# Window attention and a Fourier layer in one pipeline: mode products split around the value product, modes loaded behind them, the next image loaded in two halves

## The chip, the cores and the metric

The kernel runs on one core of a Trainium2 chip. The metric is the time of one execution in microseconds on the device, as a median of several runs; lower is better. Everything is float32.

## The reference

The input is 32 images of 56 x 56 tokens with 128 channels. Two residual layers follow each other.

```python
# group norm without scale, 32 groups of 4 channels, over a whole image
def _gn(v, G=32, eps=1e-5): ...

# layer 0: shifted-window attention, windows of 7 x 7, 4 heads
x = x + attention(_gn(x))       # qkv, scores + bias + mask, softmax, values, projection

# layer 1: Fourier layer and a feed-forward net
def _forward_fourier(x, w0, w1):
    x_fty = dct(x along the width)                       # 56 -> the first 32 modes
    out_y = einsum('bixy,ioy->boxy', x_fty[..., :32], w0)    # one 128 x 128 product per mode
    xy = idct(out_y, back to 56)
    # ... the same along the height with w1 gives xx
    return xx + xy
x = x + relu(_forward_fourier(_gn(x)) @ W1 + b1) @ W2 + b2   # 128 -> 512 -> 128
```

## The kernel before

The program is unrolled. It goes through `cycle`s; one cycle handles one row of eight windows of an image (8 rows per image), and beside it the work of older rows and of the Fourier layer of the image before. `fourier(cycle)` gives the images in that layer with a number `c`; the text calls `c` modulo 8 the row. The row's parts on TensorE in order of time:

```python
def fourier(cycle):
    b, c = divmod(cycle - CONV_BEGIN, NWR)          # CONV_BEGIN = 11, NWR = 8
    return [(images[b - k], c + k * NWR) for k in (1, 0) if 0 <= b - k < NB]

# one cycle of the steady state
halves_first(cycle, norm)      # attn_qk; load_modes for this row; ff_in; softmax division
if not has_ff(cycle):          # only row 3 has no feed-forward group
    half_columns(cycle)        # transforms or mode products
eighths(cycle)                 # attn_values of row cycle-3 (L493)
quarters(cycle)                # attn_scores (L424), then modes_back (L709)
full(cycle)                    # attn_transpose of two rows (L468, even cycles), next image's groups (L269)
halves_last(cycle, norm)       # attn_v (L402); half_columns if has_ff; next_begin; ff_out; attn_project
```

What `half_columns` does depends on the row: row 0 transforms along the width (L636), rows 1 and 2 along the height (L636), row 3 holds the four groups of mode products of the height (`mix(im, False, g)`, `w1sb`), rows 4 and 5 two groups each of the width (`mix(im, True, g)`, `w0sb`). The modes come back through a DRAM scratch: `load_modes` and `modes_back` stand in rows 4 and 5 for the height, in 6 and 7 for the width.

```python
def half_columns(cycle):
    for im, c in fourier(cycle):
        ...
        elif c == 3:
            for g in range(4):
                mix(im, False, g)
        elif c in (4, 5):
            for g in (2 * c - 8, 2 * c - 7):
                mix(im, True, g)

def mix(im, width, g):
    ...
    pz = conv_bank()
    # 8 products of one mode each (L670), into one PSUM bank
    z = work.tile([P, 4, C], F32, tag="z", name="z", bufs=3)
    nc.scalar.copy(z.rearrange("p k c -> p (k c)"), pz)                    # L678
    for u in range(2):
        nc.sync.dma_start(im.zscr[width][:, u, 4 * g : 4 * g + 4], z[...])  # L680

def load_modes(im, width, g):
    zT = work.tile([P, 4, C], F32, tag="zT", name="zT", bufs=2)
    nc.sync.dma_start(zT[:, : n // 4], im.zscr[width][l0 : l0 + n]...)     # L691, needs all four mixes
```

PSUM has eight banks, four for the attention (`attn_bank`, tag `pa`) and four for the Fourier layer (`conv_bank`, tag `pc`). In each row the attention takes its banks for queries, keys, values, scores and transposes in turn:

```python
def attn_max(r):      # VectorE maximum (L442), then on GpSimd a = a - mx (L443)
def attn_divide(r):   # VectorE sum (L454), reciprocal (L456), then on GpSimd a = a * rs (L457)
def attn_transpose(im, i, r):
    for hf in range(2):
        pt = attn_bank()
        # 4 transposes of a_sb[r % 3] into pt (L468)
        if hf: nc.scalar.copy(aT, src)             # L476
        else:  nc.vector.tensor_copy(aT, src)      # L478
def attn_values(im, i, r):
    po = [attn_bank(), attn_bank()]
    # products (L493), then po[1] + bias by VectorE in three pieces (L524), po[0] + bias by ScalarE (L526)
def attn_scores(im, i, r):
    ps = [attn_bank(), attn_bank()]
    # products (L424), then a = ps + bias and mask by VectorE, twice (L432)
```

The next image is loaded where `next_begin` calls `image_begin` (row index 3 of the attention, which is row 0 of the Fourier layer), 28 chunks in all, into one of two buffers:

```python
def load_image(b):
    t = big.tile([TC, NCH, C], F32, tag="xl", name="xl", bufs=2)
    h = NCH // 2
    for n0, n1 in ((0, h), (h, NCH)):
        for a, e, p, src in chunks_of(x, b, n0, n1):
            nc.sync.dma_start(t[p, a:e], src)
    return t
```

Its first transposes stand two rows later (`image_groups`, the first half of the chunks in row 2, the second in row 3). The order of the four compute engines is that of the program; the order of DMAs on the SyncE queue (SP) is left to the scheduler, which works from what is ready.

Of the kernel before, what the change touches and what calls it, by code (L numbers as in the profile page):

```python
# [31 lines left out]
NCH = NT // TC  # L32
# [16 lines left out]
def swin_fourier_kernel(  # L49
# [20 lines left out]
    nc = tc.nc  # L70
    NB = x.shape[0]
# [14 lines left out]
    def conv_bank():  # L86
        return bank("pc", 4)
# [3 lines left out]
    def chunks_of(t, b, n0, n1):  # L91

        tok = t[b].rearrange("h w c -> (h w) c")
        wrap = (S - SS) // 2
        if n0 < wrap:
            e = min(n1, wrap)
            part = tok[SS * S + n0 * TC : SS * S + e * TC].rearrange("(n p) c -> p n c", p=TC)
            yield n0, e, slice(0, TC), part
        if n0 <= wrap < n1:
            yield wrap, wrap + 1, slice(0, S), t[b, S - 1].unsqueeze(1)  # L100
            yield wrap, wrap + 1, slice(S, TC), t[b, 0].unsqueeze(1)
        if n1 > wrap + 1:
            a = max(n0, wrap + 1)
            t0 = (2 * a + SS) % S * S
            part = tok[t0 : t0 + (n1 - a) * TC].rearrange("(n p) c -> p n c", p=TC)
            yield a, n1, slice(0, TC), part
# [5 lines left out]
            nc.tensor.matmul(dst[ps], lhsT=lhsT[:, ps], rhs=rhs, start=start, stop=stop)  # L112


    def load_image(b):
        t = big.tile([TC, NCH, C], F32, tag="xl", name="xl", bufs=2)
        h = NCH // 2
        for n0, n1 in ((0, h), (h, NCH)):
            for a, e, p, src in chunks_of(x, b, n0, n1):
                nc.sync.dma_start(t[p, a:e], src)  # L120
        return t

    xls = {0: load_image(0)}


# [28 lines left out]
    with nc.allow_non_contiguous_dma(reason="relative position bias, once"):  # L154
# [4 lines left out]
        for ix in range(WS):  # L159
            src = bass.AP(  # L160
                rpb_rev.tensor, rpb_rev.offset + WS - 1 - ix, [[span, NH * span], [1, WS]]
            )
# [42 lines left out]
    with nc.allow_non_contiguous_dma(reason="constant, once"):  # L205
        for blk in range(8):
# [4 lines left out]
            src = idct_h.rearrange("p (h r) -> p h r", r=4)[modes, :, 2 * li : 2 * li + 2]  # L211
# [39 lines left out]
    def image_begin(b):  # L251
        im = Image()
        im.b = b
        im.x = xls.pop(b) if b in xls else load_image(b)
        im.xw, im.aT = {}, {}
        im.st = small.tile([P, NWR, 6], F32, tag="st0", name="st0", bufs=2)
        im.part = small.tile([TC, 2, C // 4, NWR], F32, tag="part", name="part", bufs=1)
        im.scr = dram.tile([S, S, C], F32, tag="scr", name="scr", bufs=2)
        return im
# [401 lines left out]
    def mix(im, width, g):  # L661

        y, wmix = (im.yw, w0sb) if width else (im.yh, w1sb)
        if g == 0:
            im.zscr[width] = dram.tile([S, 2, NM // 2, C], F32, tag="zscr", name="zscr", bufs=3)
        pz = conv_bank()
        for c in range(4):
            for u in range(2):
                k = 8 * g + 2 * c + u
                nc.tensor.matmul(  # L670
                    pz[u * JP : (u + 1) * JP, c * C : (c + 1) * C],
                    lhsT=y[:, k * S : k * S + JP],
                    rhs=wmix[:, k],
                    start=True,
                    stop=True,
# [4 lines that stand above are left out]
            nc.sync.dma_start(  # L680
                im.zscr[width][:, u, 4 * g : 4 * g + 4], z[u * JP : u * JP + S]
            )
# [5 lines left out]
    def load_modes(im, width, g):  # L688
        l0, n = LINES[g]
        zT = work.tile([P, 4, C], F32, tag="zT", name="zT", bufs=2)  # L690
        nc.sync.dma_start(  # L691
            zT[:, : n // 4],
            im.zscr[width][l0 : l0 + n].rearrange("(m r) u k c -> (r u k) m c", r=4),
        )
        im.zT[width, g] = zT
# [114 lines left out]
    images = {}  # L810

    def row(r):
        return (images[r // NWR], r % NWR) if 0 <= r < NB * NWR else (None, 0)

    def fourier(cycle):

        b, c = divmod(cycle - CONV_BEGIN, NWR)
        return [(images[b - k], c + k * NWR) for k in (1, 0) if 0 <= b - k < NB]

    def back_groups(c):  # L820

        if c in (4, 5, 6, 7):
            return [(c >= 6, c % 2 * 2 + j) for j in range(2)]
        return []

    def halves_first(cycle, norm):
        last, j = row(cycle - 4)
        if last:
            sums = attn_sums(last, j)
            next(sums)  # L830
        im, i = row(cycle)
        if im:
            attn_qk(im, i, False)
        for im, c in fourier(cycle):
            for width, g in back_groups(c):
                load_modes(im, width, g)
        next(norm)
        if last:
            next(sums)
        for im, c in fourier(cycle):  # L840
            if c == 0:
                im.stats = fourier_stats(im)
                im.cols = {}
                next(im.stats)
                load_columns(im, 0)
                load_columns(im, 1)
        for im, c in fourier(cycle):
            if c in FF_AT:
                ff_in(im, FF_AT.index(c))
        for im, c in fourier(cycle):  # L850
            if c == 0:
                next(im.stats)
        if row(cycle - 1)[0]:
            attn_divide(cycle - 1)

    def has_ff(cycle):
        return any(c in FF_AT for _, c in fourier(cycle))

    def half_columns(cycle):
        for im, c in fourier(cycle):  # L860
            if c == 0:
                for g in range(4):
                    transform(im, True, g)
            elif c in (1, 2):
                for g in (2 * c - 2, 2 * c - 1):
                    transform(im, False, g)
                    if c == 1:
                        load_columns(im, g + 2)
            elif c == 3:
                for g in range(4):  # L870
                    mix(im, False, g)
            elif c in (4, 5):
                for g in (2 * c - 8, 2 * c - 7):
                    mix(im, True, g)

    def quarters(cycle):
        im, i = row(cycle)
        if im:
            attn_scores(im, i, cycle)
        for im, c in fourier(cycle):  # L880
            for width, g in back_groups(c):
                modes_back(im, width, g)
# [22 lines left out]
    def last_out(cycle):  # L905
        for im, c in fourier(cycle):
            if c in FF_AT:
                ff_out(im, FF_AT.index(c))

    def halves_last(cycle, norm):  # L910
        im, i = row(cycle)
        if im:
            attn_v(im, i, cycle)
        if has_ff(cycle):
            half_columns(cycle)
        next_begin(cycle)
        next(norm)
        im, j = row(cycle - 3)
        if im:
            last_out(cycle)  # L920
            attn_project(im, j)
        if row(cycle)[0]:
            attn_exp(cycle)
        next(norm)

    def next_begin(cycle):
        b, i = divmod(cycle, NWR)
        if b + 1 < NB and i == 3:
            images[b + 1] = image_begin(b + 1)

# [37 lines left out]
    def nothing():  # L970
        while True:
            yield

    ET = mybir.EngineType
    with tc.manual_schedule(engines={ET.PE, ET.Activation, ET.DVE, ET.Pool}):
        images[0] = image_begin(0)
        for i in range(0, NWR, 2):
            image_groups(images[0], i)
        for _ in image_norm(images[0]):
            pass  # L980
        norm = nothing()
        for cycle in range(NB * NWR + CONV_BEGIN + FF_AT[-1] - NWR + 1):
            if cycle < CONV_BEGIN:
                first_rows(cycle, norm)
            else:
                halves_first(cycle, norm)
                if not row(cycle - 3)[0]:
                    half_columns(cycle)
                    last_out(cycle)
                    quarters(cycle)  # L990
                    continue
                if not has_ff(cycle):
                    half_columns(cycle)
                eighths(cycle)
                quarters(cycle)
                if row(cycle)[0] and cycle % 2:
                    attn_max(cycle)
                full(cycle)
                halves_last(cycle, norm)
            b, i = divmod(cycle, NWR)  # L1000
            norm = nothing()
            if i == NWR - 2 and b + 1 < NB:
                norm = image_norm(images[b + 1])
                next(norm)
# [62 lines left out]
```

## Time and profile before

| | |
|---|---|
| time, median of 3 | 3709.89 us (3704.5 to 3718.54) |
| span of the profiled execution | 3721.3 us |
| busy: TensorE / VectorE / ScalarE / GpSimd | 96% / 59% / 57% / 37% |
| mean granted TensorE clock | 0.993 |
| DMA, mean over the span | 105 GB/s |
| one image in the middle (row 0 to row 0) | about 115 us, from 1800.1 to 1915.7 us |

In the profile's lines PE is a matmul on TensorE, PEld its weight load, DVE VectorE, ACT ScalarE, POOL GpSimd, and SPq the queue of DMAs that SyncE issues. Each line of the timeline gives the start in us, the duration, the engine, the line of the kernel (L468), the operation, what is written and read, and in brackets the idle time of the engine before it and what ended it. A line of waits gives the waiting engine and tile, the releaser, the total in us, how often, and the longest. "issue" stands for idle time that no semaphore explains. The row of an instruction is found from its kind: `w1sb` is row 3, `dct_w` row 0, and so on.

### The profile page before, as it was taken

What the parts mean: (1) busy time and instruction counts of PE and PEld (TensorE: products, weight loads), DVE (VectorE), ACT (ScalarE), POOL (GpSimd) and SP (SyncE); (2) the same over time, 40 slices, a digit from 0 to 9 for tenths busy, and PEclk for the clock granted to TensorE, in tenths of its full rate; (3) what the DMA queues carried; (4) which work ended last, traced back from release to release, by engine and by line L of the source; (5) the groups of instructions that cost most, each with busy time, mean ns of one, the idle gap of its engine ahead of it and who ended that gap; (6) DMA issues with size and microseconds to landing.
All of it is one profiled execution on the core that took longest, in us unless ns stands there. A gap on an engine that the chain in (4) does not pass through costs nothing.

```text
span 3721.3 us, 161472 instructions
## 1 busy us (share of the span) xinstructions
PE 3575.8 (96%) x72064; PEld 2850.6 (77%) x72064; DVE 2209.7 (59%) x4738; ACT 2139.4 (57%) x4044; POOL 1371.3 (37%) x1421
## 2 busy tenths in 40 slices
PE   7899999999999999999999999999999999999999
PEld 5777777777777777778777877777777777777776
DVE  6765666565665666665656665566556666565641
ACT  4565556555555655556555565555555565655544
POOL 5443333343333333333333334333333334343321
PEclk9999999999999999999999999999999999999999
DMA  4334433444433343334334343433433433443333
GB/s 112 96 103 108 110 99 101 107 112 107 112 97 106 106 112 106 105 94 108 106 104 109 92 119 102 104 103 100 110 105 107 112 103 96 108 113 101 91 106 105
DMA packets 687350, 390.30 MB, mean 105 GB/s; under 512 B 39967, under 2 KB 657600, under 8 KB 686400
## 3 DMA queue, kind: packets, MB, share of 16 engines
q1 hardware_dynamic: 686045, 379.65, 37.7%
q8 instruction: 567, 9.29, 1.0%
q14 instruction: 127, 1.04, 0.1%
q10 hardware_dynamic: 611, 0.32, 0.0%
HBM read 218.29 MB, written 161.48 MB: 102 GB/s over the span
## 4 chain that ended last, share of the span: by engine, by line
PE 83%; DMA 7%; issue 2%; DVE 2%; POOL 2%; ACT 2%; SPq 1%; POOLq 0%; ACTq 0%; DVEq 0%
PE pc L112 34%; PE pa L112 13%; PE pa L402 6%; PE pa L468 6%; PE pc L636 5%; PE pa L424 4%; PE pc L709 4%; PE pc L670 4%; PE pa L493 4%; DMA zT<-zscr 4%; PE pa L269 2%; DMA zscr<-z 2%; POOL xl L300 2%; DMA out_dram<-res 1%; DVE a L432 1%
## 5 line engine op out<-in xcount | busy, mean ns | idle before, releaser
L457 POOL TENSOR_TENSOR a<-a,rs 128x784 f32<-128x784 f32 x256 | 389.7, 1522 | 1265.4 <-DVE rs L456 731.2
L112 PE MATMUL pc<-wff,hid 128*64 128x128 f32 x12544 | 745.2, 274 | 1.3 <-ACT hid L754 1.0
L112 PE MATMUL pc<-xf,wff 128*64 128x512 f32 (+2 forms) x3584 | 718.2, 539 | 0.6 <-DVE xf L720 0.6
L112 PEld LDWEIGHTS pc<-wff,hid 128*64 128x64 f32 x12544 | 707.8, 138 | 7.9 <-ACT hid L754 4.3
L778 DVE TENSOR_TENSOR res<-pc,res 128x512 f32<-128x512 f32 (+3 forms) x257 | 144.1, 571 | 910.9 <-issue 463.0
L443 POOL TENSOR_TENSOR a<-a,mx 128x784 f32<-128x784 f32 x256 | 389.8, 1522 | 662.8 <-DVE mx L442 623.8
L754 ACT ACTIVATE hid<-pc,b1sb 128x512 f32<-128x512 f32 (+2 forms) x896 | 538.3, 635 | 94.0 <-PE pc L112 91.9
L112 PEld LDWEIGHTS pc<-xf,wff 128*64 128x64 f32 x3584 | 286.0, 137 | 361.5 <-issue 281.1
L373 ACT ACTIVATE q<-pa,bqkv 128x392 f32<-128x392 f32 x256 | 149.7, 585 | 452.6 <-PE pa L112 451.0
L112 PE MATMUL pa<-xw,wn 128*64 128x392 f32 (+1 forms) x2048 | 393.9, 499 | 0.6 <-DVE a L432 0.6
L409 ACT COPY v<-pa 128x512 f32<-128x512 f32 x256 | 151.4, 591 | 269.6 <-PE pa L402 269.5
L742 POOL TENSOR_TENSOR res<-res,b2sb 128x512 f32<-128x512 f32 (+2 forms) x256 | 264.6, 1039 | 106.4 <-DMA res<-scr 96.9
L390 DVE TENSOR_SCALAR k<-pa,heads,bqkv 128x392 f32<-128x392 f32 x245 | 167.9, 685 | 213.4 <-ACT k L382 174.9
L300 POOL TENSOR_TENSOR xl<-xl,bproj 112x512 f32<-112x512 f32 (+1 forms) x256 | 287.1, 1144 | 0.0
L449 ACT ACTIVATE a<-a 128x784 f32<-128x784 f32 x256 | 222.2, 868 | 111.9 <-POOL a L443 109.7
L402 PE MATMUL pa<-wn,xw 128*64 128x128 f32 x4096 | 284.8, 281 | 0.2 <-issue 0.2
L468 PE MATMUL pa<-ident,a 113*113 113x113 f32 x2048 | 243.9, 272 | 39.6 <-ACT oT L526 38.1
L493 PEld LDWEIGHTS pa<-aT,v 49*32 49x32 f32 x16384 | 172.0, 105 | 139.0 <-issue 69.4
L432 DVE TENSOR_TENSOR a<-pa,bm 128x392 f32<-128x392 f32 x512 | 264.3, 558 | 16.3
L468 PEld LDWEIGHTS pa<-ident,a 113*113 113x113 f32 x2048 | 218.6, 181 | 60.7 <-issue 43.9
L112 PE MATMUL pa<-wproj,oT 128*64 128x128 f32 (+1 forms) x3584 | 249.0, 274 | 0.4 <-DVE oT L524 0.4
L454 DVE TENSOR_REDUCE sm<-a 128x16 f32<-128x784 f32 x256 | 245.8, 960 | 5.8 <-ACT a L449 4.9
(89 smaller groups left out, 5586.6 us busy)
## 6 DMA issues: line engine op xcount, KB each, us to landing
zscr<-z SPq DMA_DIRECT2D x512, 112.0 KB
htok<-scr SPq DMA_DIRECT2D x256, 196.0 KB
zT<-zscr SPq DMA_DIRECT2D x192, 256.0 KB
res<-scr SPq DMA_DIRECT2D x160, 256.0 KB
out_dram<-res SPq DMA_DIRECT2D x160, 256.0 KB
scr<-xl SPq DMA_DIRECT2D x128, 224.0 KB
xl<-in_x_dram SPq DMA_DIRECT2D x32, 784.0 KB
xl<-in_x_dram SPq DMA_DIRECT2D x32, 672.0 KB
```

The source lines that it names most:

```text
L112: nc.tensor.matmul(dst[ps], lhsT=lhsT[:, ps], rhs=rhs, start=start, stop=stop)
L300: nc.gpsimd.tensor_tensor(piece, piece, bproj.unsqueeze(1).to_broadcast([TC, e - a, C]), ALU.add)
L402: nc.tensor.matmul(pv[hs, j * C : (j + 1) * C], lhsT=im.xw[i][:, w * WT : w * WT + JP], rhs=im.w[:, 2 * C : 3 * C], start=True, stop=True,)
L432: nc.vector.tensor_tensor(a[:, 2 * hp : 2 * hp + 2, :, 0:WT].rearrange("p u w j -> p w u j"), ps[hp][:, :RT].rearrange("p (w u j) -> p w u ...
L443: nc.gpsimd.tensor_tensor(a3, a3, mx.unsqueeze(2).to_broadcast([P, 2 * NWR, WT]), ALU.subtract)
L449: nc.scalar.activation(a3, a3, AF.Exp)
L454: nc.vector.tensor_reduce(sm, a3, axis=AX.X, op=ALU.add)
L457: nc.gpsimd.tensor_tensor(a3, a3, rs.unsqueeze(2).to_broadcast([P, 2 * NWR, WT]), ALU.mult)
L468: nc.tensor.transpose(pt[:PW, h * P : h * P + PW], a[:PW, h, 2 * hf : 2 * hf + 2].rearrange("p w j -> p (w j)")[:, :PW], ident[:PW, :PW],)
L493: nc.tensor.matmul(po4[u][h * HD : (h + 1) * HD, 2 * f + e], lhsT=v[ks, 2 * f + e, h * HD : (h + 1) * HD], rhs=im.aT[i][f][ks, h, e * JP : ...
L742: nc.gpsimd.tensor_tensor(res[:m, c0:c1], res[:m, c0:c1], b2sb[:m].unsqueeze(1).to_broadcast([m, c1 - c0, C]), ALU.add,)
L754: nc.scalar.activation(hf[:, :n], ph[:, :n], AF.Relu, bias=b1sb[:, f : f + 1])
```

## The change

Three things are done. First, in the one row without a feed-forward group (row 3) only two of the four mode products stay ahead of the attention's values and scores; the other two move behind the value product (`attn_v`), so that the copies and stores of z come in two batches. Second, `load_modes` of the next row is written right behind the mode products, ahead of the feed-forward output and the projection with their stores, instead of at the beginning of the next row. Third, the next image's load is cut: the first half at the old place, the second half a row later.

```diff
-    def load_image(b):
+    def load_part(t, b, k):
+        h = NCH // 2
+        for a, e, p, src in chunks_of(x, b, k * h, (k + 1) * h):
+            nc.sync.dma_start(t[p, a:e], src)
+
+    def load_image(b, parts=2):
         t = big.tile([TC, NCH, C], F32, tag="xl", name="xl", bufs=2)
-        h = NCH // 2
-        for n0, n1 in ((0, h), (h, NCH)):
-            for a, e, p, src in chunks_of(x, b, n0, n1):
-                nc.sync.dma_start(t[p, a:e], src)
+        for k in range(parts):
+            load_part(t, b, k)
         return t
@@ image_begin
-        im.x = xls.pop(b) if b in xls else load_image(b)
+        im.half = b not in xls
+        im.x = load_image(b, 1) if im.half else xls.pop(b)
@@
+    def load_back(cycle):
+        for im, c in fourier(cycle):
+            for width, g in back_groups(c):
+                load_modes(im, width, g)
@@ halves_first
-        for im, c in fourier(cycle):
-            for width, g in back_groups(c):
-                load_modes(im, width, g)
@@
-    def half_columns(cycle):
+    def half_columns(cycle, rest=False):
         for im, c in fourier(cycle):
+            if rest and c != 3:
+                continue
@@
             elif c == 3:
-                for g in range(4):
-                    mix(im, False, g)
+                for g in range(2):
+                    mix(im, False, g + 2 * rest)
@@ halves_last, behind attn_v
         if has_ff(cycle):
             half_columns(cycle)
+        half_columns(cycle, True)
+        load_back(cycle + 1)
         next_begin(cycle)
@@ next_begin
         if b + 1 < NB and i == 3:
             images[b + 1] = image_begin(b + 1)
+        if b + 1 < NB and i == 4 and images[b + 1].half:
+            load_part(images[b + 1].x, b + 1, 1)
@@ the last rows, without attention
                     half_columns(cycle)
+                    half_columns(cycle, True)
                     last_out(cycle)
                     quarters(cycle)
+                    load_back(cycle + 1)
```

## The prediction

> **What bounds the kernel now.** I read the page first, then TensorE's waits, then the timeline of one image in the middle (1800 to 1916 us), first TensorE's lines and then the DMA queue's (SP).
>
> ```profile
> span 3721.3 us, 161472 instructions
> PE 3575.8 (96%) x72064; PEld 2850.6 (77%) x72064; DVE 2209.7 (59%) x4738; ACT 2139.4 (57%) x4044; POOL 1371.3 (37%) x1421
> ...
> PE pa L468 <- ACT oT L526: 38.1, 32, 2.5
> PE pc L709 <- DMA zT<-zscr: 37.3, 34, 2.6
> PE pc L636 <- issue: 24.9, 21, 2.3
> ```
>
> TensorE is busy for 96% of the span, so only its idle 145 us (3721.3 - 3575.8) can be won without taking work away, and the change takes none away. Three waits hold 100 of these, each about once per image: in row 3 the attention transposes (L468) wait 38.1/32 = 1.2 us, put down to an oT copy of ScalarE; in row 6 the inverse transform (L709) waits 37.3/34 = 1.1 us for its modes from DRAM; in row 0 the first transform (L636) stops for 24.9 us in all, and no semaphore explains that. The first two are what the change can reach, 75.4 us together, 2.0% of the span. The timeline of row 3 tells how the first comes about:
>
> ```profile
> 1840.64 3.66 PE L670 MATMUL pc<-w1sb,y 128*64 128x128 f32 x64
> ...
> 1842.99 0.36 SPq L735 DMA_DIRECT2D res<-scr  x1
> 1843.44 4.13 SPq L680 DMA_DIRECT2D zscr<-z  x8
> ...
> 1844.03 1.52 POOL L457 TENSOR_TENSOR a<-a,rs 128x784 f32<-128x784 f32 x1 [4.64 <-DVE rs L456]
> ...
> 1845.91 1.04 DVE L432 TENSOR_TENSOR a<-pa,bm 128x392 f32<-128x392 f32 x2
> 1846.23 0.59 ACT L678 COPY z<-pc 128x512 f32<-128x512 f32 x1 [2.16 <-DMA zscr<-z]
> 1846.71 0.46 ACT L526 ACTIVATE oT<-pa,bqkv 128x196 f32<-128x196 f32 x1
> ...
> 1847.31 1.81 PE L468 MATMUL pa<-ident,a 113*113 113x113 f32 x16 [1.44 <-ACT oT L526]
> ```
>
> Four mode products follow each other and z has three buffers. The fourth copy waits 2.16 us until the first store to zscr has landed (issued at 1843.44, behind a load of res that held the queue); the oT copy stands behind it on ScalarE, and the transposes need the PSUM bank that oT reads. The queue's timeline tells the same of row 6:
>
> ```profile
> 1878.98 2.34 SPq L680 DMA_DIRECT2D zscr<-z  x4
> 1882.36 0.94 SPq L798 DMA_DIRECT2D out_dram<-res  x2
> 1883.51 0.42 SPq L691 DMA_DIRECT2D zT<-zscr  x1
> 1884.03 0.44 SPq L547 DMA_DIRECT2D scr<-xl  x1
> 1884.52 0.49 SPq L691 DMA_DIRECT2D zT<-zscr  x1
> ...
> 1889.37 1.00 PE L709 MATMUL pc<-idctw,zT 64*64 64x112 f32 x32 [1.30 <-DMA zT<-zscr]
> ```
>
> The second load of modes went out behind two stores of results and a store to scr (224 KB), and landed 4.7 us after its issue (1889.24 in the chain of waits, 0.13 us before the products start).
>
> **What the Trainium skill says.** "DMA: Bandwidth & Descriptors", section "Anatomy of one DMA", puts the fixed part of a DMA at about 2 us, most of it the receipt of the write. The trace agrees: the chain has 2.23 us for a zscr store. Store and load in a row thus cost two such latencies, which sets how late a product may stand ahead of its inverse transform. "TensorE: Matmul & The Clock Gate", part 1, says that idling lets the clock fall to half for windows of about 3.4 us. The trace agrees: after a wait of 2.48 us in row 3 the windows view gives a granted clock of 0.50 from 1616.5 to 1619.8, and the 16 transposes took 3.33 us instead of 1.81. "Runtime: NRT & Kernel Launch", section "Instruction fetch mechanics", says that an engine fetches its instructions in 16 KiB blocks by DMA. Queue q8 shows 9.29 MB in 567 packets, 16 KB each; so I take the unexplained stop in row 0, in the midst of two column loads (DMA share 1.08 and 0.97 in the microseconds before), for a late block. That is an inference.
>
> **The change part by part.** *Row 3, products split.* Half the products (64 matmuls from 1840.64 to 1844.24 are 3.60 us, so 1.80) move behind the value product. Only two copies to z precede oT on ScalarE, and the third and fourth find buffers sent long before, so the 2.16 us wait and with it all of the 1.2 us go. But the attention now reaches its transposes 1.80 us earlier against chains that do not move. In the image shown scores would end at 1845.87 - 1.80 = 1844.07. GpSimd's division L457 still ends at 1844.03 + 1.52 = 1845.55, because VectorE's sums set it and those hang on the row's start; the second eight transposes read its result. VectorE's reciprocal still ends at 1843.88; its three oT pieces (0.67) and the two additions (1.04), which free the banks of the scores, then end at 1845.6 at best. The first eight transposes (half of 1.81, 0.9) are done by 1844.97, so TensorE waits some 0.65 us. Behind that VectorE needs 2.04 us for copy, maximum, copy (1847.97 to 1850.01 now), so until 1847.7; the image transposes use the same banks, and the value product waits for ScalarE's copies of them. I put 0.3 us more there. Saved: 1.2 - 0.65 - 0.3 = 0.25 us per image, 8 us over 32, and not 38. Three half-clock windows in row 3 (rows with waits of 2.1 to 2.5 us) go as well, about 1.5 us each from the transposes above: 5 us.
>
> *Row 4, modes loaded late.* The fourth product now ends about 0.9 us (the projection) before row 4 begins. Its copy ends 0.8 us after it (0.2 to start, 0.59). In the image shown the zT load came 2.9 us after that copy (1846.82 to 1849.69), and by the windows view both loads' bytes were through about 3 us later. The sum is 6.7 us after the product. Available are the projection 0.9, row 4's start to the inverse transform 6.3 (1852.42 to 1858.73), and 0.75 more for the second group: 7.2 and 7.9 us. There is 0.5 to 1.2 us of room, to be eaten up in some images by a late queue (store to load varies by about 1.5 us over the images). I charge 0.2 us per image: 6 us lost.
>
> *Row 6, modes loaded behind the products.* The queue does not keep the program's order: in the trace row 4's loads were issued at 1849.69, ahead of row 3's store to scr at 1853.41, though written behind it. What the change alters is precedence among DMAs that are ready. Both zT loads then go ahead of the 224 KB store and perhaps of the results. With row 4's 3 us from issue to both through, they land at 1883.5 + 3.1 = 1886.6, before 1887.12, where the transform begins. I count 34 of the 37.3 us as gone, and one half-clock window (2 us).
>
> *Image in two halves.* The same 1456 KB and small pieces move. TensorE waits for that load only at the start (7.8 us, 2 times), so nothing is won directly. If the second half runs behind the column loads of row 1, up to 1.5 MB lie in a row ahead of row 2's short attention products, where a late instruction block could stop TensorE as in row 0. I charge 3 us. Row 0's 24.9 us stay: its column loads and its products are not touched.
>
> Sum: -8 - 5 + 6 - 34 - 2 + 3 = -40 us. From 3709.9 that is 3670 us.
>
> **The rivals.** (1) The waits simply go, all 75 us with their clock windows: about 3630 us. For it: each is one event with one cause. Against it: the division and the additions in row 3, which end at times that the split does not move. (2) Row 4 takes over the wait: with 1 us too little room per image 32 us come back, and the time is near 3700. For it: two DMA latencies stand in the path now. Against it: 3.6 us of feed-forward lie between. (3) The queue keeps its old order since readiness decides it, and the halves are sent back to back: then only row 3 counts, about 3700 us. Against it: the second zT load was plainly ready at 1884.03. (4) Moved traffic makes new late instruction blocks: 1 us in each image would be 32 us, about 3700.
>
> **Range and chances.** The two gains are capped at 75 us plus about 10 of clock; the likeliest losses are rivals 2 and 4. I put 8 chances in 10 on 3640 to 3700. Faster by over 2% means under 3635.7, which needs all of rival 1: 5%. Slower by over 2% would need 2.3 us lost per image on top of the gains: 2%. Within 2%: 93%.
>
> **What would show it.** Right: the wait of L468 for oT falls from 38 us, with waits for the division (POOL a), the additions (DVE a) or ScalarE's copies in its stead, some 0.6 to 1 us per image; ScalarE's wait for zscr (52.1 us) falls below 10; zT waits of L709 fall under 10 us in all and stand in row 4; L636's stop stays near 25 us. Wrong: row 3 shows no new wait (then 20 to 30 us more are won), L709 waits over 0.5 us per image in row 4, row 6 still waits, or stops without a cause rise in rows 1 and 2.

## The result, and the profile after

The changed kernel takes 3674.1 us (median of 4 runs, 3666.7 to 3677.5), the kernel before 3709.1 us: a ratio of 0.990, interval 0.9875 to 0.9925, 35 us less. The prediction was 3670.

The page of the changed kernel begins so; the engine line has busy us, share of the span and number of instructions.

```profile
span 3664.9 us, 161414 instructions
...
PE 3567.3 (97%) x72064; PEld 2845.5 (78%) x72064; DVE 2196.4 (60%) x4738; ACT 2138.8 (58%) x4044; POOL 1370.4 (37%) x1421
```

The instructions on the engines are the same in number, and TensorE's busy time is 8.5 us shorter; its idle time fell from 145 to 98 us (3664.9 - 3567.3). (The code has moved by four lines: L468 is now L472, L636 L640, L709 L713, L457 L461.) TensorE's waits, as before (total us, times, longest):

```profile
PE pc L640 <- issue: 20.5, 20, 1.8
PE pa L472 <- POOL a L461: 14.5, 32, 0.5
PE pc L713 <- DMA zT<-zscr: 12.1, 17, 3.1
```

ScalarE's wait for a z buffer, in the kernel before and in this one:

```profile
ACT z L678 <- DMA zscr<-z: 52.1, 34, 3.2
```

```profile
ACT z L682 <- DMA zscr<-z: 1.0, 1, 1.0
```

The 38.1 us of the transposes for oT are gone, and in their place stand 14.5 us for GpSimd's division: 32 times, 0.45 us each. ScalarE's wait for zscr fell from 52.1 to 1.0 us. The wait for modes fell from 37.3 to 12.1 us, of which 6.7 us now stand in row 4 (0.2 before). The stop of the first transform, 20.5 us, stays: it lies between 19 and 28 us in every kernel here that leaves the column loads at their place. The timeline of row 3 in one image:

```profile
1815.82 1.49 PE L112 MATMUL pa<-xw,wn 128*64 128x392 f32 x8
...
1819.72 0.90 PE L428 MATMUL pa<-k,q 64*64 64x98 f32 x32
1819.82 0.45 ACT L530 ACTIVATE oT<-pa,bqkv 128x196 f32<-128x196 f32 x1
...
1820.53 1.52 POOL L461 TENSOR_TENSOR a<-a,rs 128x784 f32<-128x784 f32 x1 [4.65 <-DVE rs L460]
1820.56 1.08 PE L472 MATMUL pa<-ident,a 113*113 113x113 f32 x8
...
1822.10 1.04 PE L472 MATMUL pa<-ident,a 113*113 113x113 f32 x8 [0.46 <-POOL a L461]
1822.98 1.73 PE L273 MATMUL pa<-ident_x,xl 112*128 112x112 f32 x14
...
1824.64 1.09 PE L406 MATMUL pa<-wn,xw 128*64 128x128 f32 x16
```

oT leaves ScalarE at once (1819.82), and the first eight transposes start when the scores end. The second eight start 0.05 us after the division's end (1820.53 + 1.52 = 1822.05), which stands 6.23 us behind the row's start, as before (1845.55 - 1839.33 = 6.22; the row's start before is this line):

```profile
1839.33 1.49 PE L112 MATMUL pa<-xw,wn 128*64 128x392 f32 x8
```

A chain that does not move has become the bound. The queue, from row 5's stores to row 6's loads, and the inverse transform that reads them:

```profile
1854.73 2.15 SPq L684 DMA_DIRECT2D zscr<-z  x4
1858.10 0.94 SPq L802 DMA_DIRECT2D out_dram<-res  x2
1859.26 0.96 SPq L695 DMA_DIRECT2D zT<-zscr  x2
1860.31 0.46 SPq L551 DMA_DIRECT2D scr<-xl  x1
...
1862.87 1.71 PE L713 MATMUL pc<-idctw,zT 64*64 64x112 f32 x64
```

Both loads of modes now go ahead of the store to scr, still behind the results; the inverse transform of this image ran its 64 products without a wait.

The table gives the mean length of a row over the 29 or 30 full images of each trace, worked out as the distance between the first query products of two rows:

| row | before, us | after, us | difference |
|---|---|---|---|
| 3 (split) | 12.96 | 12.30 | -0.66 |
| 4 (modes loaded late) | 14.96 | 15.18 | +0.22 |
| 6 (modes loaded early) | 11.43 | 10.36 | -1.07 |
| 0 | 16.00 | 15.71 | -0.29 |
| 1, 2, 5, 7 together | 58.63 | 58.72 | +0.09 |
| all eight | 113.99 | 112.27 | -1.72 |

1.72 us times 32 is 55 us, about the difference of the two spans (56) but not of the medians (35). The two profiled executions stand at opposite ends: the one before, 3723 us, had seven half-clock windows in these images (three in row 3, three in row 0, one in row 6), the one after, the fastest of its four runs, had none. Row 3's -0.66 holds such windows; its median went from 12.85 to 12.36, -0.49. Row 0's -0.29 is no gain of the change: it is three such windows and 4.4 us fewer stops.

### The profile page after: what moved, and what is told of

Same layout as the page of the kernel before. It is cut to its first block, busy times and chain, and to the rows that moved or that the text cites. A ratio compares the mean times of both kernels' runs of the same rounds, so it can differ in the third digit from the quotient of the medians.

```text
span 3664.9 us, 161414 instructions
## 1 busy us (share of the span) xinstructions
PE 3567.3 (97%) x72064; PEld 2845.5 (78%) x72064; DVE 2196.4 (60%) x4738; ACT 2138.8 (58%) x4044; POOL 1370.4 (37%) x1421
## 4 chain that ended last, share of the span: by engine, by line
PE 89%; DVE 3%; DMA 3%; POOL 2%; ACT 2%; issue 2%; SPq 0%; ACTq 0%; POOLq 0%; DVEq 0%
PE pc L112 36%; PE pa L112 14%; PE pa L406 7%; PE pc L640 6%; PE pa L472 5%; PE pc L713 5%; PE pa L428 5%; PE pc L674 5%; PE pa L497 4%; PE pa L273 3%; DMA zT<-zscr 2%; POOL a L461 1%; DVE sm L458 1%; ACT k L386 1%; DVE k L394 1%
## 5 line engine op out<-in xcount | busy, mean ns | idle before, releaser
L461 POOL TENSOR_TENSOR a<-a,rs 128x784 f32<-128x784 f32 x256 | 389.6, 1522 | 1264.8 <-DVE rs L460 761.4
L472 PE MATMUL pa<-ident,a 113*113 113x113 f32 x2048 | 249.7, 272 | 15.6 <-POOL a L461 14.5
L480 ACT COPY aT<-pa 113x452 f32<-113x452 f32 x256 | 139.8, 546 | 213.3 <-PE pa L472 213.3
L472 PEld LDWEIGHTS pa<-ident,a 113*113 113x113 f32 x2048 | 218.8, 179 | 40.7 <-POOL a L461 20.9
```

Source lines behind the costliest of these rows:

```text
L461: nc.gpsimd.tensor_tensor(a3, a3, rs.unsqueeze(2).to_broadcast([P, 2 * NWR, WT]), ALU.mult)
L472: nc.tensor.transpose(pt[:PW, h * P : h * P + PW], a[:PW, h, 2 * hf : 2 * hf + 2].rearrange("p w j -> p (w j)")[:, :PW], ident[:PW, :PW],)
```

## The experiments

Theory: the split trades the wait for ScalarE's fourth copy for a shorter one on the division; the loads' precedence is worth the wait of row 6; the halves do nothing. The first three runs take the parts alone; ratios are to the kernel before on the same chip (3730 us there), with the 95% interval in brackets. The diffs are shortened and against the changed kernel, that of the fourth buffer against the kernel before; where the image is loaded in one piece, the second `load_part` is left out too.

**Only the split.**

```diff
 # of the change, kept: range(2), mix(im, False, g + 2 * rest)
-        load_back(cycle + 1)             # behind the products
+        load_back(cycle)                 # in halves_first, as before
-        im.x = load_image(b, 1)
+        im.x = load_image(b)
```

> Only the split of the four mode products in row 3; modes loaded at the next row's start as before, image in one piece. My theory (row 3's wait is replaced by a shorter one for GpSimd's division; row 4 has little room): row 3 wins 0.5 to 0.65 us per image, row 4 loses up to 0.5 us since the store of row 3 now goes ahead of the loads of modes: 0 to 20 us faster, about 3698, and row 6 still waits some 37 us. Rival (the split is the whole gain): 30 us or more faster.

0.9959 (0.9940 to 0.9977), 15 us. Its waits:

```profile
PE pc L713 <- DMA zT<-zscr: 48.4, 43, 3.3
PE pc L640 <- issue: 23.0, 19, 2.1
PE pa L472 <- POOL a L461: 14.5, 32, 0.5
```

oT is gone and the division is there, as in the whole change, while the wait for modes grew from 37.3 to 48.4 us: 11 us of the gain went into the modes, 8 of them in row 4, whose mean grew by 0.31 us. Row 6 still waits 37.5 us. So the theory's first half holds.

**Only the loads' place.**

```diff
-                for g in range(2):
-                    mix(im, False, g + 2 * rest)
+                for g in range(4):           # and no second part
+                    mix(im, False, g)
-        im.x = load_image(b, 1)
+        im.x = load_image(b)
```

> Only the loads of modes written right behind the mode products; four products together in row 3, image in one piece. My theory: row 6's wait of 37 us goes to under 10, row 3's wait for oT stays near 38 us, so 30 to 36 us faster, about 3676. Rival (the queue's order is set by readiness, the place in the program does not matter): no change, 3709.

0.9897 (0.9854 to 0.9941), 35 us.

```profile
PE pa L472 <- ACT oT L530: 37.7, 31, 2.8
PE pc L640 <- issue: 24.4, 19, 2.0
...
PE pc L713 <- DMA zT<-zscr: 6.4, 9, 1.6
```

The wait for modes fell by 31 us, and the other two large waits stayed. The place in the program does decide among DMAs that are ready.

**Only the halves.**

```diff
-                for g in range(2):
-                    mix(im, False, g + 2 * rest)
+                for g in range(4):
+                    mix(im, False, g)
-        load_back(cycle + 1)
+        load_back(cycle)                 # in halves_first
```

> Only the image in two halves. My theory: nothing, since no wait of TensorE hangs on that load and the queue sends most of the second half straight behind the first: within 5 us of 3709. Rival (spreading the load relieves instruction blocks and stores): 10 us or more faster, with L636's stop of 25 us in row 0 reduced.

0.9988 (0.9972 to 1.0003), 4 us of 3730, not told from nothing. The timeline of the changed kernel's queue says what the cut became there (row 0 and row 1 of one image):

```profile
1895.05 1.13 SPq L118 DMA_DIRECT2D xl<-in_x_dram  x2
1899.24 0.40 SPq L802 DMA_DIRECT2D out_dram<-res  x1
1899.79 0.39 SPq L551 DMA_DIRECT2D scr<-xl  x1
1900.23 1.64 SPq L118 DMA_DIRECT2D xl<-in_x_dram  x3
```

The first two are the 784 KB half and 672 KB of the other; only the three small pieces were put behind the stores. Nothing holds the second half back, so the scheduler sends it at once.

**The whole change but the halves**, at first beside the three parts, then beside the changed kernel and a kernel where the second half is truly held back:

```diff
-        im.x = load_image(b, 1) if im.half else xls.pop(b)
+        im.x = load_image(b) if im.half else xls.pop(b)      # without halves
```

```diff
         if b + 1 < NB and i == 4 and images[b + 1].half:
-            load_part(images[b + 1].x, b + 1, 1)
+            t = images[b + 1].x
+            nc.scalar.copy(t[:, NCH // 2 :, 0], bproj[:, : NCH // 2])   # held back
+            load_part(t, b + 1, 1)
```

> The whole change but for the image, which is loaded in one piece. My theory: the same as the changed kernel, 3670 to 3678. Rival (the halves bring part of the gain): over 10 us slower than that.

> The changed kernel once more, on the same chip as the next three: 0.985 to 0.990 of the kernel before.

> The changed kernel with the image in one piece, beside the changed kernel. My theory (the halves bring nothing, since the queue sends 672 of the second 784 KB right behind the first half): within 0.3% of the changed kernel. Rival (the halves help or harm): apart by more than that.

> The changed kernel where the second half of the image is really held until row 1's transforms are done (a copy of 14 values per partition by ScalarE into its buffer). If the halves brought nothing only because the queue undid them: some gain now, 3 to 10 us, by fewer stops without a cause. If no wait of TensorE hangs on the image: within 5 us of the changed kernel.

| kernel | ratio to before | interval | range of runs, us |
|---|---|---|---|
| without halves, first chip | 0.9848 | 0.9813 to 0.9884 | 3669.7 to 3679.9 |
| changed kernel again | 0.9895 | 0.9879 to 0.9911 | 3671.1 to 3680.6 |
| without halves again | 0.9868 | 0.9854 to 0.9882 | 3662.0 to 3669.0 |
| halves held back | 0.9876 | 0.9861 to 0.9891 | 3663.1 to 3672.8 |

The last three share a chip (before: 3717 us). The parts add up: split, loads and halves alone took 0.41, 1.03 and 0.12%, the first two together 1.52 and 1.32%. By medians the first two together are 51 us faster than before on both chips, their sum alone 50. The halves add nothing to these; in the one direct comparison the kernel without them is 9.6 us faster (0.26%, inside the 0.3% I had set; the times of single runs do not overlap, the 95% intervals do, barely). The two traces have images of 112.5 us each and do not show where; that stays open. With the second half held back the kernel is 6.3 us faster than the changed kernel, inside the 3 to 10 us that I had put on a gain, but their runs overlap, and the kernel without the halves is faster still. So no gain of the halves is shown, held back or not.

**A fourth buffer in place of the split.** If the copy's wait is all that row 3 suffers from, a buffer cures it without bringing the transposes forward. The hidden layer's buffers are idle in row 3, and one of them serves as the fourth z.

```diff
-        z = work.tile([P, 4, C], F32, tag="z", name="z", bufs=3)
+        if width or g < 3:
+            z = work.tile([P, 4, C], F32, tag="z", name="z", bufs=3)
+        else:
+            z = work.tile([P, HB], F32, tag="hid", name="zh", bufs=NF)   # seen as P x 4 x C
```

> The kernel before, where the fourth mode product of row 3 is copied into a buffer of the hidden layer that is idle in that row, so that it waits for no store; nothing else changed. If row 3's wait comes from that copy alone, it goes without a successor (the transposes stay behind all four products): L468's 38 us go to under 5, and with the half-clock windows of that row the time falls by 35 to 45 us, to about 3668. Rival (the transposes wait for something that only the copy hides, a bank or the division): a wait of 0.4 us or more per image stays and the gain is under 25 us.

> Loads of modes right behind the products, and the fourth buffer in place of the split. Both waits should go with none in their place, and row 4 has its old room: 70 to 80 us faster than before, about 3632, which is some 40 us faster than the changed kernel. Rival (the gains overlap): not faster than the changed kernel by more than 15 us.

On the kernel before: 0.9901 (0.9879 to 0.9923), 37 us; with the loads behind the products 0.9812 (0.9797 to 0.9826), 72 us (before: 3723 us). The waits of the first:

```profile
PE pc L712 <- DMA zT<-zscr: 39.0, 33, 2.8
PE pc L636 <- issue: 24.3, 19, 2.3
...
PE pa L468 <- POOL a L457: 0.3, 1, 0.3
```

Row 3's wait has no successor: its transposes stand behind all four products, and the division is done by then. Row 3 has a mean of 11.82 us, against 12.30 with the split, and row 4 keeps its old 14.97. The gains of buffer and loads add (37 + 35 = 72). Against the changed kernel that is some 31 us by ratios from two chips, where I had put 40.

**Row 0's stop.** The prediction inferred a late block of instructions. The trace has the packets of the queues that fetch them; q8 moved 90% of their bytes, and TensorE has 89% of the instructions (144128 of 161472), so I take q8 for TensorE's. This view covers 1917.2 to 1918.6 us of the kernel before, where a stop begins that lasts from 1917.64 to 1919.90 (packets, MB, share of the 16 DMA engines' time):

```profile
q8 instruction: 1, 0.02, 5.5%
q1 hardware_dynamic: 17, 0.01, 2.1%
```

That one 16 KB packet ran from 1917.32 to 1918.54. In all 20 stops over 0.3 us in these products in the trace of before, TensorE resumed 1.32 to 1.62 us after such a packet had ended, while the packets come some 6 us apart (median), so this is not chance. To see whether the column loads are what delays it, they were held behind row 0's transforms:

```diff
-                load_columns(im, 0)          # halves_first of row 0
-                load_columns(im, 1)
@@ half_columns, behind row 0's four transforms
+                load_columns(im, 0, True)
+                load_columns(im, 1, True)
@@ load_columns
+        if late:
+            nc.scalar.copy(t[:, 0, 0:1], im.yw[:TC, 0:1])    # t waits for the transforms
```

> The changed kernel, where the first two column loads (784 KB) go out behind row 0's transforms (a copy of one element by ScalarE into their buffers holds them back). If row 0's stop is an instruction block held up by those loads, L636's 20.5 us fall under 5 and the time falls by 15 to 20 us, to about 3656. Rival (the stop has another cause at that place): it stays near 20 us and the time does not move; or the stop turns up in row 1, where the loads now lie.

> Loads behind the products, fourth buffer in place of the split, and late column loads. If all three causes hold: about 3615, 95 us faster than before. If the late loads only move the stop: about 3632.

> Loads behind the products, fourth buffer in place of the split, late columns, and the second half of the image held back. Before this, with late columns, 6 us of stops had moved into row 1, where columns and the whole image lie together. If the mass of that traffic makes them: the stops in row 1 fall to under 3 us and the time to 0.974 of the kernel before. If not: 0.977 as without the holding back.

Late columns on the changed kernel: 0.9824 (0.9808 to 0.9841), where the changed kernel has 0.9895: 0.71% or some 26 us, but by ratios from two chips. The one pair on the same chip, loads and buffer without and with late columns, gives 3651.4 and 3635.3: 16 us or 0.4%, and the traces of the changed kernel without and with them differ by 0.5 us per image, 17 us. So 16 us is the better figure; I had put 15 to 20. Its waits:

```profile
PE pa L472 <- POOL a L461: 14.1, 31, 0.5
...
PE pc L640 <- issue: 5.9, 7, 1.5
PE pc L640 <- DMA htok<-scr: 4.3, 2, 3.6
```

All 5.9 us are row 1's: row 0's transforms run without a stop. Row 0 fell to a mean of 14.88 us with next to no spread, while row 1 rose from 15.20 to 15.41: most of the stop went, a part moved to where the loads now lie. All three cures together gave 0.9766 (0.9751 to 0.9782), 88 us where I had put 95. With the image's second half held back besides, 0.9751 (0.9738 to 0.9764), 3621.3 us against 3717.2, where 0.974 was expected. Of the stops in the transforms this is left:

```profile
PE pc L640 <- issue: 0.2, 1, 0.2
```

Without the holding back it was 6.4 us in 8 stops. So the mass of loads in row 1 made those; the time, though, is not told apart from 0.9766 by the intervals. This last kernel, without the split, is 54 us faster than the changed kernel on the same chip (3675.8).

## Why the prediction was right

The sum (-40; measured -35, and -41 by the medians on another chip) was right with the mechanism, and two of its terms were mis-sized, in opposite directions: row 3 won about 8 us more than predicted, and the halves, by one comparison, cost some 7 us more. That the sum came this close is in part luck.

- *The wait that takes the place.* Predicted: 0.65 us for the division, additions behind it. Measured: 0.46 us shown as a wait, and the first eight transposes took 1.08 us where I had put 0.9, so most of the 0.65 is there. Rival 1 (all 75 us go) fell on this.
- *Another 0.3 us in row 3* behind VectorE's copies was wrong. From the image transposes to the value product it is 1.66 us (1822.98 to 1824.64), no more than before (1848.97 to 1850.62, 1.65). So row 3 won about 0.5 us per image where I had 0.25: 16 us for 8.
- *Half-clock windows.* The seven windows of the profile before are gone, but that is one execution: traces of the parts alone have six or seven, those of later kernels none to three. My 7 us for four of them is neither shown nor refuted by the times. The Trainium skill ("TensorE: Matmul & The Clock Gate", part 1) has the clock fall after an idle window of about 3.4 us; in the trace of before, the seven half-clock windows of 3.41 us came right behind shorter waits, of 1.80 to 2.48 us, while others of 2.14 to 2.56 us were followed by none.
- *Row 4.* Predicted +0.2 us per image, the table has +0.22. The room was as thin as worked out: 6.5 us more of waits for modes stand in this row. Rival 2 (a full microsecond) fell; the split alone, where the loads keep their old place, lost more (0.31). In all, though, the waits for modes are 12.1 us, where the sign of being right was under 10.
- *Row 6.* Predicted 34 us, that is 1.06 per image; measured 1.07 in the traces and 35 us for the loads alone. Rival 3 fell: readiness comes first, but among the ready the program's order counts.
- *Image halves.* Predicted as +3 us through new stops. The queue sent the second half at once, so the premise of that term, a load a row later, did not come about. What the runs show is none alone (0.9988) and, beside the other parts, a loss of 9.6 us in one comparison, whose cause stays open. Rival 4 (new late blocks, 1 us in each image) fell: the stops without a cause outside row 0 rose from 5 to 12 us, most of it in row 6 and not in rows 1 and 2, where I looked for it.
- *Two readings.* The stop in row 0 is not "about once per image": it is 21 stops in 32 images. And the 2 us that the Trainium skill ("DMA: Bandwidth & Descriptors", section "Anatomy of one DMA") gives for the fixed part of a DMA stand there for DMAs that GpSimd issues; these are issued by SyncE, so it is the 2.23 us of the trace that carries the argument.

## What to carry to other kernels

When a burst of work fills a ring of buffers, look for what stands behind the blocked copy on the same engine: here it was the oT copy, not z, that TensorE waited for. Moving work to break up such a burst brings other work forward against chains that do not move; here a buffer that another stage leaves idle removed the wait without a successor and won more than twice as much (37 us against 15). And a DMA "moved" in this program was only moved where something made it wait: precedence among the ready was worth 35 us, cutting a load without a dependency won nothing.

## What the runs showed of the hardware

In row 0 the stops of TensorE that no semaphore explains were late instruction blocks: in 20 of 20 cases it resumed 1.3 to 1.6 us after a 16 KB packet of its fetch queue had ended. They came where 784 KB of loads ran beside short products, cost 19 to 28 us per run, and vanished from that row when those loads were held behind the products. The Trainium skill ("Runtime: NRT & Kernel Launch", section "Instruction fetch mechanics") calls the cost of such a block boundary mostly hidden. By number that holds here: of 567 blocks 28 stopped TensorE for over 0.2 us. But these stops came to 30 us in the kernel before, those of row 0 were TensorE's third largest wait, and a cure by placement was worth about 16 us, 0.4%.
